# A two-layer token model on one Trainium2 core: values with d on partitions, the norm applied on each head's way out, and a second half whose x stays turned

## The chip, the core and the metric

The program runs on one core of a Trainium2 chip. The metric is device time in microseconds (us) from launch to end, as the median of three runs: 1463.49 us for the kernel before (1462.98 to 1463.92). All data is 32-bit floating point. Engines are named as in the profile: PE (TensorE, matmuls), PEld (TensorE's weight loads), DVE (VectorE), ACT (ScalarE), POOL (GpSimd) and SP (SyncE, which here only issues DMAs).

## The reference, cut to what matters

`x` is 64 batches of 32 tokens with 256 features. Four blocks are added to it in turn. The change touches the first, part of the second, and the third.

Layer 0 attention, for 16 heads of width 128, on `hs = x` mixed by a small matrix per batch:

```python
W2 = where(mask, einsum('bhtm,bhjm->bhtj', qv * enz, es), 0)
o = einsum('bhtj,bhjd->bhtd', W2, v)                    # values
g = hs @ Wg.T
o_n = o * rsqrt(mean(o * o, -1) + 1e-5) * g_norm_weight  # norm over d, one number per token and head
o_g = o_n * silu(g)
x = x + o_g.reshape(B, T, H * 128) @ Wo.T               # all heads summed
```

The norm's factor is one number per token and head, so it commutes with the product by `Wo` of that head.

The second block is a gated MLP with adapters of each batch (rank 16, 8 adapters), then a gated MLP with ternary weights, added to `x`. The third is a linear layer with an adapter of each batch, then attention with 16 heads of width 16:

```python
e = x @ W.T + s[idx] * ((x @ A[idx].T) @ Bm[idx].T)     # rank 16, 8 adapters
q, k, v = split(e @ W_qkv + b_qkv)                      # 16 heads x 16, rotary on the first 4
x = x + softmax(q k^T / 4, causal) v @ W_dense + b_dense
```

The fourth is a product by an expert's matrix of each batch, and a MLP with values rounded to 8-bit steps.

## The kernel before

Tokens are handled in eight chunks of 256 (8 batches, two groups of 128 tokens). The order of the work is written out by hand (`manual_schedule`): each engine takes its instructions in the order in which the Python code emits them. All PSUM results use one pool of eight banks of 128 x 512 (`bank()`); a bank is taken again when the last instruction that uses it, as emitted, is done, and the one released first is taken first.

**First half: `turn(n)`.** Layer 0 attention is cut into 32 steps: 4 groups of four heads, times 8 chunks. `turn(n)` weaves together three or four steps at different stages: `scores`, `attend` and `weigh` of step n; `slots_exp`, `cumsum` and the projections (`project_qk`, L700; `project_vg`, L731) of step n+1 or n; `mix`, `values`, `norm`, `gate`, `turn_og` of step n-1; `leave` of step n-2. What concerns us:

- `values` (L913): the product `w2T^T v`, in 16 matmuls of a 64 x 64 array tile with 128 columns of `v` moving. The result has tokens on partitions and d along the free axis. ACT squares each head and sums along d with `accum_out` (L922).
- `norm` (L929, L931): DVE adds the epsilon, POOL takes the power -1/2 (`f2`).
- `gate` (L943): eight DVE instructions of 128 x 128, each o times `f2` times the gate.
- `turn_og` (L953): eight transposes on PE, and six ACT copies (L957, L960), so that d lies on partitions for the next product.
- `leave` (L968, L973): eight matmuls with 256 moving columns, four heads accumulated in one bank half, and one DVE add of 128 x 512 into `x`.
- `project_vg` for the gate: tokens on partitions, four matmuls of 512 moving columns, and six ACT instructions with Silu.

Beside them, `prepare` (L197 and around) rounds weights for the last block, and `tabulate` copies the adapters of the second block into two tables in DRAM, `alora` and `blora`, from which POOL's indirect DMAs gather each batch's own. `load_mlp` loads the second half's first weights into slots as the attention weights leave them; `chunk_0` runs the start of the second half inside the last turns.

**Second half: `turn2(n)`.** Turn n works on chunk n (adapters, `gate_up`, `down`, `ffn_up`, `ffn_down`, `linear_in`, `linear_adapters`, `linear`), on chunk n-1 (`qkv`, `turn_qk`, `attn_scores`, `attn_exp`, `attn_weights`, `attn_values`, `attn_out`) and on chunk n-2 (`experts_in`, `run_experts`, the last MLP). `drain` finishes chunks 6 and 7. `x` has tokens on partitions, so three times per chunk four PE transposes (L342, through `turned`) turn it: `tokens_in`, `linear_in`, `experts_in`. The linear layer's adapters are all eight at once: `linear_adapters` (L543) multiplies by all 128 ranks, and a DVE multiply with a 0/1 table leaves each batch its own. `qkv` (L1098) makes q, k and v together with tokens on partitions; `turn_qk` (L1136) turns q and k by eight PE transposes.

The weights of the second half (`lw`, `qkvw`, `qkvb`, `dw`, `db`) lie in memory that the first half holds; SP issues their five DMAs when the first half is over (834.5 to 836.9 us).

Of the kernel before, what the change touches and what calls it, by code (L numbers as in the profile page):

```python
# [15 lines left out]
P = 128  # L16
# [9 lines left out]
for _name, _n in (  # L26
    ("ident", 128), ("pair", 64), ("cos", 32), ("sin", 32), ("cos4", 4),
    ("sin4", 4), ("causal", 32), ("blk4", 4), ("adapter", 1), ("p_mod32", 1), ("p", 1), ("p_mod16", 1),
    ("row16", 1), ("head2", 2), ("out_row", 1),
):  # L30
    _CONST[_name] = (_NCONST, _NCONST + _n)
    _NCONST += _n
# [6 lines left out]
def _constants():  # L39
# [25 lines left out]
    put("adapter", p // 16)  # L65
# [10 lines left out]
def mk_kernel(  # L76
# [65 lines left out]
    tables = {}  # L142
    fold = keep.tile([P, P], F32, tag="fold", name="fold")

    def small_tables():
# [20 lines left out]
        m6 = keep.tile([P, B], F32, tag="m6", name="m6")  # L166
        tables["m6"] = m6
        nc.vector.tensor_scalar(m6, idx("lora2"), const("adapter"), scal, ALU.is_equal, MULT)
# [105 lines left out]
    def load_mlp(part):  # L274

        if part == 0:

            for i in range(2):
                mlp["ag", i] = slot(f"ag{i}", [P, 1024])
            mlp["la"] = load(  # L280
                mlp["ag", 0][:, 768:].rearrange("p (c f) -> p c f", c=2),
                laT.rearrange("(c p) f -> p c f", p=P),
            )
            mlp["lbt"] = load(mlp["ag", 1][:, 768:], lb)
        names = {0: (("cgt", 0), ("cut", 0), ("bx", 0)), 1: (("bx", 1), ("cgt", 1)), 2: (("cut", 1), ("cdt", 0))}
        for key in names.get(part, (("cdt", 1),)):
# [8 lines left out]
            else:  # L295
# [3 lines left out]
                    src[:, i * 512 : (i + 1) * 512].rearrange("(c p) f -> p c f", p=P),  # L299
# [4 lines left out]

    alora = dram.tile([8 * P, 192], F32, tag="alora", name="alora")

    blora = dram.tile([8 * P, 2 * P], F32, tag="blora", name="blora")

    def tabulate():
        to = alora.rearrange("(a p) v -> p a v", p=P)  # L310
        pieces = [(ag, k, k * 32) for k in range(2)] + [(au, k, k * 32 + 16) for k in range(2)]
        pieces += [(ad, k, 64 + k * 16) for k in range(8)]
        for src, k, lo in pieces:
            with nc.allow_non_contiguous_dma(reason="ranks of an adapter"):
                nc.sync.dma_start(
                    out=to[:, :, lo : lo + 16], in_=src[k * P : (k + 1) * P, :].rearrange("p (a i) -> p a i", i=16)
                )
            yield
        for r in range(4):
# [36 lines left out]

    def tokens_in(ch):
        c = chunks[ch]
        c["xT"] = turned(lambda gi, k: xq[ch][:, gi, k * P : (k + 1) * P], "xT", first, 2)
# [27 lines left out]
    def fetch_down(ch, gi, held=True):  # L387

        g = ch * 2 + gi
        gather(bdt[:, gi, :], bd, didx[:, g : g + 1], held)  # L390

# [129 lines left out]
    def ffn_down(ch):  # L521
        c = chunks[ch]
        ps = bank()
        for k in range(6):
            for gi in range(2):
                nc.tensor.matmul(  # L526
                    ps[:, gi * D : (gi + 1) * D], lhsT=c["gT"][:, k, gi * P : (gi + 1) * P],
                    rhs=f2w[:, k, :], start=(k == 0 and gi == 0), stop=(k == 5 and gi == 1),
                )
        x = xq[ch].rearrange("p g f -> p (g f)")  # L530
        nc.vector.tensor_tensor(x, ps, x, ADD)

    def linear_in(ch):
        c = chunks[ch]
        c["xT"] = turned(lambda gi, k: xq[ch][:, gi, k * P : (k + 1) * P], "xT", first, 2)

        nc.gpsimd.tensor_tensor(xq[ch], xq[ch], db.unsqueeze(1).to_broadcast([P, 2, D]), ADD)

    def linear_adapters(ch):
        c = chunks[ch]  # L540
        ps = bank()
        for k in range(2):
            nc.tensor.matmul(  # L543
                ps[:, :256], lhsT=mlp["la"][:, k, :], rhs=c["xT"][:, k, :], start=(k == 0), stop=(k == 1)
            )
        xa = big.tile([P, 256], F32, tag="xa", name="xa")
        nc.vector.tensor_tensor(by_batch(xa), by_batch(ps[:, :256]), of_batch(tables["m6"], ch), MULT)
        c["xa"] = xa

    def linear(ch):  # L550
        c = chunks[ch]
        ps = bank()
        for i in range(2):
            for k in range(2):
                nc.tensor.matmul(
                    ps[:, i * 256 : (i + 1) * 256], lhsT=lw[:, k, i * P : (i + 1) * P],
                    rhs=c["xT"][:, k, :], start=(i == 0 and k == 0), stop=False,
                )
        for i in range(2):
            nc.tensor.matmul(  # L560
                ps[:, i * 256 : (i + 1) * 256], lhsT=mlp["lbt"][:, i * P : (i + 1) * P], rhs=c["xa"],
                start=False, stop=(i == 1),
            )
        eT = big.tile([P, 2, 256], F32, tag="eT", name="eT", bufs=2)
        nc.scalar.copy(eT.rearrange("p c t -> p (c t)"), ps)
# [3 lines left out]
    with ExitStack() as s1:  # L569
# [155 lines left out]
        def project_vg(i, which):  # L725
            hq, q, w, hs, lo, s = at(i)
            wt = w[2 if which == "v" else 3]
            for gi in range(2):
                ps = bank()
                for c in range(2):  # L730
                    nc.tensor.matmul(  # L731
                        ps, lhsT=hs[:, c, lo + gi * P : lo + (gi + 1) * P], rhs=wt[:, c, :],
                        start=(c == 0), stop=(c == 1),
                    )
                t = work.tile([P, 512], F32, tag=which, name=which, bufs=2)
                if which == "v":
                    nc.scalar.copy(t, ps)
                else:
                    to, of = by_parity(t), by_parity(ps)
                    nc.scalar.activation(to[:, :, 0, :], of[:, :, 0, :], AF.Silu)  # L740
                    for half in range(2):
                        here, there = slice(half * 64, half * 64 + 64), slice(64 - half * 64, P - half * 64)
                        nc.scalar.activation(to[here, :, 1, :], of[there, :, 1, :], AF.Silu)
                s[which, gi] = t
# [842 lines left out]
```

## Time and profile before

| | us |
|---|---|
| median of three runs | 1463.49 |
| the profiled execution's own time | 1462.34 |
| its span, first to last instruction | 1460.6 |
| PE busy in the span | 1411.5 (97%) |
| PEld / DVE / ACT / POOL busy | 1082.4 / 827.1 / 617.0 / 514.4 |
| one turn of the first half (718.20 to 741.53) | 23.33 |
| one turn of the second half (1080.31 to 1158.10) | 77.79 |
| mean granted TensorE clock | 0.988 |

A row of the profile's groups names a line of the code, the engine, the tiles out<-in, the shape and the count. Every matmul of the code stands in the trace as two records (`values` has 16 matmuls in each of 32 steps, and L913 has 1024 records), a transpose as one (L953: 8 times 32 is 256). Each record has a weight load of its own (PEld). Matmuls are pipelined, so the mean of one is longer than the time from one to the next; the time that a group takes of PE is read from the start of its first record to the start of the next group's first.

### The profile page before, as it was taken

Reading aid. Unit: us, or ns where it says so; the run is one execution under the profiler, and the core shown is the slowest. Engines: PE = TensorE matmul, PEld = TensorE weight load, DVE = VectorE, ACT = ScalarE, POOL = GpSimd, SP = SyncE. Lnnn points to the kernel's source line nnn. Section 1 sums busy time; section 2 is a strip of 40 time slices with the busy share of each in tenths; the row PEclk is TensorE's granted clock in tenths of the full one; section 3 lists DMA queues with packets and bytes.
Section 4 is the critical chain, followed back from the end, with each engine's and each line's share of the span. In section 5 each row is a group of like instructions: output and inputs, shape, how many; then the busy total and the mean of one; then the engine's idle time right before and its main releaser. Section 6 shows DMA issues by size and latency. Waiting matters only on the chain.

```text
span 1460.6 us, 37036 instructions
## 1 busy us (share of the span) xinstructions
PE 1411.5 (97%) x15496; PEld 1082.4 (74%) x15496; DVE 827.1 (57%) x1899; ACT 617.0 (42%) x2014; POOL 514.4 (35%) x586
## 2 busy tenths in 40 slices
PE   5899999999999999999999999999999999999997
PEld 3666777777777777667767878788887878787865
DVE  2566677776768676667565224363636263534555
ACT  1355575656566575746566312121312121222121
POOL 3433243333424243324354243333252515152130
PEclk9999999999999999999999999999999999999999
DMA  6201010100111000100001222122221212121120
GB/s 182 55 2 66 2 30 31 34 2 12 33 39 41 9 9 12 46 2 1 13 16 50 72 79 74 52 73 59 58 75 55 78 38 84 41 73 46 43 77 18
DMA packets 61503, 65.14 MB, mean 45 GB/s; under 512 B 34901, under 2 KB 48853, under 8 KB 61337
## 3 DMA queue, kind: packets, MB, share of 16 engines
q0 software_dynamic: 13312, 35.93, 8.8%
q1 hardware_dynamic: 44824, 22.33, 5.6%
q10 hardware_dynamic: 3200, 4.52, 1.0%
q8 instruction: 122, 2.00, 0.6%
q14 instruction: 45, 0.36, 0.1%
HBM read 60.66 MB, written 3.93 MB: 44 GB/s over the span
## 4 chain that ended last, share of the span: by engine, by line
PE 92%; DMA 2%; DVE 2%; issue 2%; ACT 1%; SPq 1%; POOL 0%; DVEq 0%; POOLq 0%; ACTq 0%
PE ps L700 16%; PE ps L731 15%; PE ps L968 8%; PE ps L436 8%; PE ps L507 5%; PE ps L1301 5%; PE ps L482 3%; PE ps L1341 3%; PE ps L1098 3%; PE ps L526 3%; PE ps L913 2%; PE ps L810 2%; PE ps L450 2%; PE ps L953 2%; PE ps L888 1%
## 5 line engine op out<-in xcount | busy, mean ns | idle before, releaser
L714 POOL TENSOR_TENSOR qT<-ra,rb 128x256 f32<-128x256 f32 x64 | 46.5, 727 | 365.0 <-DVE rb L712 365.0
L922 ACT ACTIVATE sq<-ps 128x128 f32<-128x128 f32 x256 | 70.9, 277 | 213.9 <-PE ps L913 206.8
L368 POOL DMA_INDIRECT we<-in_ew,at x64 | 61.4, 960 | 255.5 <-DVE at L366 170.6
L968 PE MATMUL ps<-wo,ogT 128*128 128x256 f32 x512 | 123.3, 396 | 6.7 <-DVE aT L817 6.7
L700 PE MATMUL ps<-hsT,wq 128*128 128x256 f32 x512 | 126.5, 391 | 0.0
L700 PE MATMUL ps<-hsT,wk 128*128 128x256 f32 x512 | 121.5, 380 | 0.0
L711 DVE TENSOR_TENSOR ra<-ps,ct 128x512 f32<-128x512 f32 x128 | 87.6, 684 | 49.1 <-PE ps L700 44.1
L731 PE MATMUL ps<-wv,hsT 128*128 128x512 f32 x256 | 115.2, 593 | 0.0
L731 PE MATMUL ps<-wg,hsT 128*128 128x512 f32 x256 | 115.1, 592 | 0.0
L968 PEld LDWEIGHTS ps<-wo,ogT 128*128 128x128 f32 x512 | 97.8, 196 | 21.9 <-DVE aT L817 7.3
L700 PEld LDWEIGHTS ps<-hsT,wq 128*128 128x128 f32 x512 | 95.6, 192 | 18.3 <-issue 6.0
L794 DVE RECIPROCAL enz<-ps 128x256 f32<-128x256 f32 x64 | 107.5, 1721 | 1.5 <-PE ps L785 1.5
L700 PEld LDWEIGHTS ps<-hsT,wk 128*128 128x128 f32 x512 | 97.9, 191 | 13.4
L931 POOL TENSOR_TENSOR f<-f,mhalf 128x8 f32<-128x8 f32 x32 | 52.9, 1652 | 132.3 <-DVE f L929 132.3
L731 PEld LDWEIGHTS ps<-wg,hsT 128*128 128x128 f32 x256 | 48.7, 190 | 61.2 <-issue 54.0
L712 DVE TENSOR_TENSOR rb<-ps,ct 128x512 f32<-128x512 f32 x128 | 87.2, 681 | 0.0
L848 ACT ACTIVATE qv<-ok,nmx 128x64 f32<-128x64 f32 x256 | 84.9, 335 | 1.9 <-DVE nmx L844 1.9
L731 PEld LDWEIGHTS ps<-wv,hsT 128*128 128x128 f32 x256 | 48.6, 190 | 47.5 <-issue 45.9
L1301 PE MATMUL ps<-guT,y3T 128*128 128x352 f32 x256 | 79.6, 465 | 1.2 <-ACT y3T L347 1.2
L817 DVE SCALAR_TENSOR_TENSOR aT<-ps,ct 128x256 f32<-128x256 f32 x64 | 24.2, 419 | 86.8 <-PE ps L810 86.8
L458 DVE TENSOR_TENSOR hT<-ps,sg 128x256 f32<-128x256 f32 x64 | 24.3, 420 | 83.5 <-ACT sg L457 83.5
L507 PE MATMUL ps<-yT,f 128*128 128x256 f32 x320 | 71.2, 382 | 0.2 <-ACT yT L493 0.2
(225 smaller groups left out, 2985.3 us busy)
## 6 DMA issues: line engine op xcount, KB each, us to landing
x<-in_x SPq DMA_DIRECT2D x8, 256.0 KB, 9.4
wq<-in_wqT SPq DMA_DIRECT2D x16, 128.0 KB, 2.6
wk<-in_wkT SPq DMA_DIRECT2D x16, 128.0 KB, 3.2
wv<-in_wvT SPq DMA_DIRECT2D x4, 512.0 KB, 10.9
wg<-in_wgT SPq DMA_DIRECT2D x4, 512.0 KB, 3.9
wo<-in_woT SPq DMA_DIRECT2D x4, 512.0 KB, 4.7
row<-in_wgu ACTq DMA_DIRECT2D x11, 128.0 KB, 2.7
out<-res SPq DMA_DIRECT2D x5, 256.0 KB, 2.8
```

What stands on the lines that cost most here:

```text
L368: nc.gpsimd.indirect_dma_start(out=to, out_offset=None, in_=table, in_offset=bass.IndirectOffsetOnAxis(ap=at, axis=0))
L436: nc.tensor.matmul(ps[:, i * 256 : (i + 1) * 256], lhsT=mlp[name, k // 4][:, j, part], rhs=c["xT"][:, j, :], start=(i == 0 and j == 0), st ...
L507: nc.tensor.matmul(ps[:, i * 256 : (i + 1) * 256], lhsT=wt[:, j, k * P : (k + 1) * P], rhs=yT[:, j, :], start=(j == 0), stop=(j == 1),)
L700: nc.tensor.matmul(ps[:, half * 256 : (half + 1) * 256], lhsT=wt[:, c, half * 256 + pr * P : half * 256 + (pr + 1) * P], rhs=hs[:, c, lo : ...
L711: nc.vector.tensor_tensor(by_t(a.rearrange("p h t -> p (h t)")), by_t(ps), cosb, MULT)
L712: nc.vector.tensor_tensor(by_t(b.rearrange("p h t -> p (h t)")), by_t(ps), sinb, MULT)
L731: nc.tensor.matmul(ps, lhsT=hs[:, c, lo + gi * P : lo + (gi + 1) * P], rhs=wt[:, c, :], start=(c == 0), stop=(c == 1),)
L794: nc.vector.reciprocal(t[:, e, :], banks[e][:, :256])
L848: nc.scalar.activation(qv[:, k, :], ok[:, k, :], AF.Exp, bias=nmx[:, k : k + 1], accum_out=rs[:, k : k + 1],)
L922: nc.scalar.activation(sq, po[e][:, k * P : (k + 1) * P], AF.Square, accum_out=f[:, e * 4 + k : e * 4 + k + 1],)
L968: nc.tensor.matmul(ps[:, gi * D : (gi + 1) * D], lhsT=s["ogT", gi][:, h, :], rhs=w[4][:, h, :], start=(h == 0), stop=(h == 3),)
L1301: nc.tensor.matmul(ps[:, :352], lhsT=c["y3T"][:, k, gi * P : (gi + 1) * P], rhs=guT[:, k, lo : lo + 352], start=(k == 0), stop=(k == 1),)
```

## The change

Nothing of the result changes; the work is laid out otherwise.

First half:

- `values` swaps its operands: v is now the weight (64 rows x 128 columns of the array) and `w2T` moves, 64 columns each, so that d lies on partitions. Two ACT instructions square both halves.
- `norm` sums the squares over partitions by eight matmuls with the squares as weight and a single column of ones moving. It is emitted after `project_v`, where before it stood ahead of the last projections.
- `project_g` makes the gate with d on partitions (eight matmuls of 256 columns, two Silu instructions). `gate` multiplies o by it in two DVE instructions, without the norm, and is emitted ahead of the second pair of q/k projections. `turn_og` is gone.
- `leave` keeps heads apart in four banks; eight DVE instructions scale each head by its `f2` while they add it to `x`.

Second half:

- `tokens_in` turns x with features interleaved, and `x` then stays turned: `ffn_down` and `attn_out` produce turned results from weight columns taken with a step of two (`i::2`). `linear_in` and `experts_in` are gone; `tokens_back` turns x back once, before the last add. A third buffer holds a turned x.
- The linear layer has each batch's own adapter. `tabulate` first builds two more DRAM tables, and by 72 gathers on POOL and 24 DMAs on SP the adapters of each chunk (`own_in`, `own_out`), which `fetch_linear` loads per chunk.
- `qkv` becomes `queries_keys` (weights `eT`, 32 array columns each, 128 columns of the q/k weights moving) and `project_values`; q and k are turned by DVE's 32 x 32 transpose instead of PE, and `kb` is made half on ACT, half on DVE.
- The q/k weights are loaded in 32 DMAs of 64-byte pieces, their bias in 16, the values' in three.
- The expert gathers (`fetch`) move later in the turn, and `drain` is put in another order.

```diff
         def values(i):
-                def product(e, rows, out):
-                    nc.tensor.matmul(
-                        po[e][out, k * P : (k + 1) * P], lhsT=s["w2T"][rows, e, k, :],
-                        rhs=s["v", gi][rows, h * P : (h + 1) * P], start=True, stop=True,
-                    )
...
+            for gi in range(2):
+                for h in range(4):
+                    for half in range(2):
+                        rows = slice(64 * half, 64 * half + 64)
+                        k = gi * 4 + h
+                        nc.tensor.matmul(
+                            po[half][:, k * 64 : (k + 1) * 64], lhsT=s["v", gi][rows, h * P : (h + 1) * P],
+                            rhs=s["w2T"][rows, h % 2, gi * 2 + h // 2, :], start=True, stop=True,
+                        )
+            sq = work.tile([P, 8, 2, 64], F32, tag="sq", name="sq", bufs=1)
+            for half in range(2):
+                nc.scalar.activation(
+                    sq[:, :, half, :], po[half].rearrange("p (k t) -> p k t", k=8), AF.Square
+                )
         def norm(i):
+            for gi in range(2):
                 for h in range(4):
+                    to = h % 2 * 4 + gi * 2 + h // 2
                     nc.tensor.matmul(
+                        ps[:, to : to + 1],
+                        lhsT=s["sq"][:, gi * 4 + h, :, :].rearrange("p a t -> p (a t)"), rhs=ones[:, :1],
+                        start=True, stop=True,
                     )
...
         def gate(i):
+            for half in range(2):
+                nc.vector.tensor_tensor(
+                    to[:, half], s["po"][half].rearrange("p (g h t) -> p g h t", g=2, h=4), by[:, half], MULT
+                )
-        def turn_og(i):
...
         def leave(i):
+            for gi in range(2):
+                for pr in range(2):
+                    ps = bank()
+                    for e in range(2):
+                        h = pr * 2 + e
+                        nc.tensor.matmul(
+                            ps[:, e * D : (e + 1) * D], lhsT=s["og"][:, h, gi * P : (gi + 1) * P],
+                            rhs=w[4][:, h, :], start=True, stop=True,
+                        )
+                    for e in range(2):
+                        of = e * 4 + gi * 2 + pr
+                        nc.vector.scalar_tensor_tensor(
+                            xq[q][:, gi, :], ps[:, e * D : (e + 1) * D], s["f2"][:, of : of + 1],
+                            xq[q][:, gi, :], MULT, ADD,
+                        )
...
             more(N)
-            on(n - 1, norm)
+            on(n - 1, gate)
             on(n + 1, project_qk, "q", 1)
             on(n + 1, project_qk, "k", 1)
-            on(n - 1, gate)
             on(n, weigh)
-            on(n, project_vg, "v")
-            on(n, project_vg, "g")
+            on(n, project_v)
+            on(n - 1, norm)
+            on(n, project_g)
...
     def linear_adapters(ch):
+            for j in range(4):
+                nc.tensor.matmul(
+                    ps[32 * j : 32 * j + 32, :64], lhsT=mlp["la"][:, j, k, :],
+                    rhs=c["xT"][:, k, j * 64 : (j + 1) * 64], start=(k == 0), stop=(k == 1),
+                )
     def linear(ch):
+        for gi in range(2):
+            for i in range(2):
+                for k in range(2):
+                    nc.tensor.matmul(
+                        banks[gi][:, i * P : (i + 1) * P], lhsT=lw[:, k, i * P : (i + 1) * P],
+                        rhs=c["xT"][:, k, gi * P : (gi + 1) * P], start=(i == 0 and k == 0), stop=False,
+                    )
+        for i in range(2):
+            for gi in range(2):
+                rows = slice(64 * gi, 64 * gi + 64)
+                nc.tensor.matmul(
+                    banks[gi][:, i * P : (i + 1) * P], lhsT=mlp["lbt"][rows, i * P : (i + 1) * P],
+                    rhs=c["xa"][rows, :, :, :].rearrange("p a b t -> p (a b t)"), start=False, stop=(i == 1),
+                )
...
+    def queries_keys(ch):
+            for b in range(4):
+                for k in range(2):
+                    for i in range(4):
+                        nc.tensor.matmul(
+                            ps[32 * i : 32 * i + 32, b * P : (b + 1) * P],
+                            lhsT=c["eT"][:, k, gi * P + b * T : gi * P + (b + 1) * T],
+                            rhs=wqk[:, k, i, :, :, :].rearrange("p o s d -> p (o s d)"),
+                            start=(k == 0), stop=(k == 1),
+                        )
...
+        nc.vector.transpose(qkT.rearrange("p k s t -> p (k s t)"), flat)
+        nc.scalar.activation(kb[:, :, 0, :], qkT[:, :, 1, :], AF.Copy, scale=const("head2")[:, 0:1])
+        nc.vector.tensor_scalar(kb[:, :, 1, :], qkT[:, :, 1, :], const("head2")[:, 1:2], None, MULT)
+    def project_values(ch):
+                nc.tensor.matmul(
+                    ps[:, gi * 256 : (gi + 1) * 256], lhsT=c["eT"][:, k, gi * P : (gi + 1) * P],
+                    rhs=wv[:, k, :, :].rearrange("p h d -> p (h d)"), start=(k == 0), stop=(k == 1),
+                )
```

## The prediction, made before the result was known

> **What bounds the kernel now.** I read the page's busy shares, then busy time by stretch for one turn of the first half and one of the second, then the timeline of PE inside such a turn, then single groups for prices. Busy shares:
>
> ```profile
> PE 1411.5 (97%) x15496; PEld 1082.4 (74%) x15496; DVE 827.1 (57%) x1899; ACT 617.0 (42%) x2014; POOL 514.4 (35%) x586
> ```
>
> Busy time by stretch (length, then PE, PEld, DVE, ACT, POOL), two turns of the first half and one of the second:
>
> ```profile
> 718.20:741.53 23.33, 23.33 (x262) 17.13 (x260) 14.67 (x29) 14.63 (x53) 10.48 (x13) 1.00 0.03 10
> 741.53:764.86 23.33, 23.33 (x261) 17.13 (x260) 14.66 (x29) 14.63 (x53) 12.36 (x15) 1.00 0.08 21
> ...
> 1080.31:1158.10 77.79, 77.48 (x884) 63.35 (x883) 36.56 (x107) 16.97 (x37) 28.04 (x30) 1.00 0.22 62
> ```
>
> In a steady turn PE is busy all of 23.33 us, at full clock, and DVE, ACT and POOL have 9 us or more free; in the second half PE lacks 0.3 us of 77.79. So the time is the sum of what PE is given; relief on ACT and DVE is worth nothing by itself. The timeline of PE (start, length, line, count) prices each part by start to next start:
>
> ```profile
> 718.63 1.04 PE L953 MATMUL ps<-ct,og 128*128 128x128 f32 x8
> 719.60 0.48 PE L762 MATMUL ps<-ws,rT 17*128 17x256 f32 x2
> ...
> 722.06 3.72 PE L968 MATMUL ps<-wo,ogT 128*128 128x256 f32 x16
> 725.62 1.89 PE L700 MATMUL ps<-hsT,wq 128*128 128x256 f32 x8
> ...
> 729.17 1.10 PE L913 MATMUL ps<-v,w2T 64*64 64x128 f32 x32
> 730.09 0.64 PE L831 MATMUL ps<-es,aT 64*64 64x64 f32 x32
> ...
> 738.10 3.60 PE L731 MATMUL ps<-wg,hsT 128*128 128x512 f32 x8
> 741.53 0.27 PE L871 MATMUL ps<-ct,qe 128*128 128x128 f32 x1
> ```
>
> `turn_og`: 719.60 - 718.63 = 0.97. `values`: 0.92. `leave`: 3.56. The gate's projection: 3.43.
>
> Two more groups decide the case, the only ones with 128-column weights and less than 128 moving columns (timeline again):
>
> ```profile
> 145.97 0.28 PE L222 MATMUL ps<-part,ones 128*128 128x1 f32 x2
> ...
> 1112.64 2.01 PE L450 MATMUL ps<-u,bx 32*128 32x64 f32 x64
> 1114.59 0.56 PE L1301 MATMUL ps<-guT,y3T 128*128 128x352 f32 x1
> ```
>
> L222 is one matmul with one moving column, in two records. A lone record takes 167 ns (the minimum of the group, whose median is 208 and maximum 250), the pair 0.28 us: the second ends 0.11 us after the first although one column streams in no time. L450 has four row tiles of 32, 64 columns each: 64 records in 1114.59 - 1112.64 = 1.95 us, 0.122 us per four.
>
> **What the Trainium skill says.** "TensorE: Matmul & The Clock Gate", section "LDWEIGHTS (loading the stationary operand)": a load takes P/1.2 ns for P weight columns, whatever the rows; 128 columns are 107 ns. Both groups above agree: 0.11 and 0.122 us are a weight load, not the stream. The same page, "The mechanism": a load overlaps running matmuls only where the row groups differ; L450 agrees, since its four row tiles load side by side. "TensorEngine Tiling (Array Packing)", "Instruction Overhead": a matmul with one moving column takes as long as one with 60, so narrowing does not pay there; the 167 ns of L222 for one column fits. The same page, "Key Properties": changing the tiling mode drains the array; the timeline shows about 0.1 us at such a change (1.95 us against 16 loads of 0.112).
>
> **The change, part by part, on PE.** First half, per step:
>
> - `turn_og` leaves: 8 transposes, -0.97.
> - `norm` comes: 8 matmuls of one column, 16 records of 128-column weights, each 0.11 to 0.112: +1.79. It is not hidden: the loads are on one row group and PE has no gap.
> - `values`: again 16 matmuls, but as 64 x 128 tiles only two row groups run side by side instead of four tiles. Streaming stays equal (half the tiles, half the columns), but each tile now loads 128 columns per record: 32 records, two abreast, 16 x 0.112 = 1.79 instead of 0.92: +0.87. No row of before has this shape; the bounds are 0.92 (loads hidden) and 3.58 (no overlap at all). I take 1.79, because L450 shows row groups overlapping and the load setting the pace.
> - `project_g`: 16 records of 256 columns at 0.216 (L700: 1.73 for eight) against 3.43: +0.02. `leave`: 16 records as before, 0.
>
> Sum +1.71 per step, times 32 = +54.7 us.
>
> What else moves in a turn is hidden under PE. DVE: `leave` 8 x 0.38 (L817's shape: two in 0.76) for 0.69, `gate` 2 x 0.68 for 2.15, `e2` three small ones for one: about +1.8 on 14.67 of 25.0. ACT loses six copies, four Silu parts and six squares. POOL's power comes after `qe`, which helps `turn_qe`: `qe` has only 0.24 us in hand before PE needs it (741.29 against 741.53), and about 1 us after. The added wait is PE's on the squares, and `norm` stands 9 us behind `values`. The banks of `leave` were last read by `aT` and `w2T` on DVE, done 1 us earlier. `tabulate` adds 9 gathers of about 1 us in eight turns on POOL, in its idle stretch between `qe` and the next q/k (11 us). If that cover fails, q/k come late by the overrun, but they serve the next turn.
>
> Second half, per chunk: `linear_in` -0.44 and `experts_in` -0.47, `tokens_back` +0.44; `linear_adapters` 0.86 becomes 16 records of 32-column weights, 64 moving, 4 groups of 0.058 and a mode change: -0.53; `linear` base 1.73 becomes 16 records at 0.112: +0.06, its adapter part 0.96 becomes 8 records in pairs, about 0.60: -0.36; `qkv` 5.26 becomes 32 groups of four at 0.11 (3.6) and 8 records of 256 (1.8): +0.14; `turn_qk` -0.87. Sum -2.03, times 8 = -16.2 us. Stepped weights (`i::2`) lie under 256 moving columns, as long as such a load stays below 0.216 (the stepped transposes of `experts_in` paid 0.118 instead of 0.109).
>
> Ends and seams: chunk 0's `linear_in` also waited 0.86, turn 7's `experts_in` 0.5; `drain` puts work into gaps where PE stood 1 us each before `attn_scores`, `attn_out` and `run_experts`: about -3. Against it, SP issues 51 DMAs at 0.35 to 0.51 us from 834.5 us, some 24 us, before `queries_keys` of chunk 0 can run; PE comes to it about 28 us after the first half ends. Landing takes 2 to 3 us, so 0 to 3 us of stall, I take 1. Together -3.5.
>
> Total: 54.7 - 16.2 - 3.5 = +35.0. Against the profiled execution: span 1460.6 + 35 = 1495.6, with 1.7 around it 1497.3; the median of before lies 1.15 above that execution, so 1498.5, said as 1498.
>
> **Rivals.**
>
> - Faster, because weight loads hide. For it: L222's two records start only 28 ns apart, and PEld is busy only 74%. If one-column records cost 0.028 and `values` keeps 0.92, a step changes by 0.45 - 0.97 = -0.5, the first half by -17, and the total is 1463.5 - 17 - 20 = 1427. Against: the ends lie 0.11 apart, and L450. It ends faster as soon as `norm` and the growth of `values` cost under 1.6 us together, instead of 2.66.
> - Half of it: `values` keeps its streaming pace, `norm` pays. Then +0.84 per step, +27 - 20 = +7: 1471.
> - Slower still: a first-half turn is no longer bound by PE alone. `mix` needs `qeT` from ACT, and the 0.97 us of `turn_og` that stood between is gone; or the array's clock drops. For it: before, the clock fell to half twice in the middle of the first half, where `mix` waited about 3 us. At 0.5 to 1 us per turn: +16 to +32, 1515 to 1530. Against: ACT has six copies less ahead of that copy.
> - The change does not do what it says for ACT and DVE: no, it does relieve them, but neither sets the time.
>
> **How the numbers follow.** Forecast 0.82 (own range 1486 to 1508, from the drain, the DMA seam and 0.1 us per step either way), hidden loads 0.05, half 0.04, slower still 0.09. The range, 1481 to 1514, adds the nearer part of the slower case. Three runs of this kernel span 0.06%; about 0.2% is what can be told from no change. Faster 0.05, within 0.2% 0.01, slower 0.94.
>
> **What would show it.** In the changed profile: the one-column group with 512 records, some 57 us busy; `values` near 1.8 us per step; a turn of about 25.0 us with PE still full; a chunk of about 75.8 us. Wrong if the one-column records follow each other in under 0.06 us, if PE shows gaps in the first half, or if a chunk does not shrink.

## The result, and the profile after

The changed kernel takes 1521.32 us (median of four runs, 1517.28 to 1523.61) beside 1463.34 us for the kernel before: ratio 1.0393, 95% interval 1.037 to 1.0415. That is +58 us; the forecast was +35, and 1521 lies above the range. The profiled execution has a span of 1519.7 us, 59.1 more than before, at the same granted clock of 0.988. In part of experiment 5 the kernel before itself took 1551 us, and what ran beside it there is compared with that.

Busy shares of the changed kernel:

```profile
PE 1463.3 (96%) x17064; PEld 1195.4 (79%) x17064; DVE 946.2 (62%) x1975; ACT 481.0 (32%) x1246; POOL 576.8 (38%) x650
```

ACT lost 136 us and the time grew: relief there was worth nothing. PE gained 52 us of busy time, weight loads 113, and DVE 119. Busy time by stretch (length, then PE, PEld, DVE, ACT, POOL), for two turns of the first half and one of the second:

```profile
749.69:774.97 25.28, 25.19 (x280) 20.45 (x276) 18.43 (x32) 10.40 (x30) 10.30 (x13) 1.00 0.04 10
774.97:800.36 25.39, 25.30 (x280) 20.52 (x276) 18.43 (x32) 10.48 (x30) 10.41 (x13) 1.00 0.04 10
1104.00:1180.22 76.22, 76.12 (x1019) 63.91 (x1022) 36.56 (x103) 16.56 (x36) 26.84 (x29) 1.00 0.23 67
```

A turn is still full of PE, and 2 us longer than the 23.33 of before; the undisturbed ones (4, 5, 25 and 26) take 25.18. A chunk of the second half is 1.57 us shorter. The timeline of PE in the first of these turns (start, length, line, count):

```profile
751.51 3.72 PE L1057 MATMUL ps<-wo,og 128*128 128x256 f32 x16
...
758.61 2.00 PE L1008 MATMUL ps<-w2T,v 64*128 64x64 f32 x32
760.54 0.69 PE L920 MATMUL ps<-es,aT 64*64 64x64 f32 x32
...
768.60 1.84 PE L1026 MATMUL ps<-ones,sq 128*128 128x1 f32 x16
770.30 3.70 PE L826 MATMUL ps<-hsT,wg 128*128 128x256 f32 x16
773.84 0.60 PE L966 MATMUL ps<-ct,qe 128*128 128x128 f32 x4
```

From start to next start: `values` 1.93 us (L1008), `norm` 1.70 (L1026), the gate's projection 3.54. The sixteen one-column records of `norm` follow each other in 1.70 / 16 = 0.106 us, although each by itself is shown as 167 to 250 ns long (shortest, median, longest):

```profile
L1026 PE MATMUL ps<-ones,sq x512: 167/250/250, 92.5 to 892.5; 128*128 128x1 f32 x171
```

Where the 59 us came from, stretch by stretch of the two profiled executions (turns are cut at the first record of `scores`, chunks at the adapters of `down`, L466 before and L537 after; the forecast is the prediction's sum, laid on the stretches):

| stretch | before | after | change | forecast |
|---|---|---|---|---|
| start to the first `scores` | 41.8 | 44.5 | +2.7 | 0 |
| turns 0 to 3 | 106.4 | 114.1 | +7.7 | +5.1 |
| turns 4 to 22 | 447.0 | 483.7 | +36.7 | +32.5 |
| turns 23 to 30 | 194.4 | 208.2 | +13.8 | +13.7 |
| rest of the first half | 44.1 | 49.5 | +5.4 | +3.4 |
| chunks 0 and 1 | 130.3 | 127.7 | -2.6 | -3.9 |
| chunks 2 to 6 | 388.9 | 381.1 | -7.8 | -10.2 |
| the last chunk and the drain | 107.7 | 110.9 | +3.2 | -5.5 |

The largest single miss is the last row. PE's waits from 1478 us to the end (who waited, for what, us in total, times, longest):

```profile
PE ps L1435 <- DVE h L204: 7.0, 1, 7.0
PE ps L1451 <- ACT h3T L1438: 1.4, 3, 0.5
```

and the timeline of PE there:

```profile
1482.85 1.93 PE L1381 MATMUL ps<-we,xT 128*32 128x256 f32 x32
1491.77 1.09 PE L1435 MATMUL ps<-ct,h 128*128 128x128 f32 x4 [6.98 <-DVE h L204]
1492.65 0.64 PE L1437 MATMUL ps<-ct,h 128*128 128x128 f32 x2
```

After `run_experts(7)` PE comes straight to `turn_h(6, 1)`, whose `quant_h(6, 1)` stands on DVE behind the rounding of both groups of `y`. PE idles 7 us, and the four transposes after it start 0.22 us apart instead of 0.11: from 1489.0 us on, 6.8 us ran at half the clock. Before, `quant_down(6, 0)` and `quant_up(7, 0)` stood between the two, and the longest waits of PE in the last 37 us were 0.9 and 0.8 us.

### The profile page after: what moved, and what is told of

Its sections match the earlier page's. It is cut to its first block, busy times and chain, and to the rows that moved or that the text cites. A ratio compares the mean times of both kernels' runs of the same rounds, so it can differ in the third digit from the quotient of the medians.

```text
span 1519.7 us, 39665 instructions
## 1 busy us (share of the span) xinstructions
PE 1463.3 (96%) x17064; PEld 1195.4 (79%) x17064; DVE 946.2 (62%) x1975; ACT 481.0 (32%) x1246; POOL 576.8 (38%) x650
## 4 chain that ended last, share of the span: by engine, by line
PE 91%; DVE 2%; SPq 2%; DMA 2%; issue 1%; ACT 1%; POOL 0%; ACTq 0%; DVEq 0%
PE ps L779 15%; PE ps L1057 8%; PE ps L826 7%; PE ps L507 7%; PE ps L809 7%; PE ps L1411 5%; PE ps L1008 4%; PE ps L578 4%; PE ps L1026 4%; PE ps L553 3%; PE ps L1451 3%; PE ps L597 2%; PE ps L899 2%; PE ps L521 2%; SPq L276 2%; PE ps L1219 2%
## 5 line engine op out<-in xcount | busy, mean ns | idle before, releaser
L1057 PE MATMUL ps<-wo,og 128*128 128x256 f32 x512 | 124.4, 398 | 7.5 <-DVE aT L906 6.0
L1063 DVE SCALAR_TENSOR_TENSOR x<-ps,f,x 128x256 f32<-128x256 f32 x256 | 120.9, 482 | 15.2 <-PE ps L1057 3.0
L826 PE MATMUL ps<-hsT,wg 128*128 128x256 f32 x512 | 118.3, 384 | 0.0
L1057 PEld LDWEIGHTS ps<-wo,og 128*128 128x128 f32 x512 | 98.5, 197 | 24.7 <-DVE aT L906 10.8
L1014 ACT ACTIVATE sq<-ps 128x512 f32<-128x512 f32 x64 | 34.8, 595 | 250.1 <-PE ps L1008 250.1
L826 PEld LDWEIGHTS ps<-hsT,wg 128*128 128x128 f32 x512 | 94.9, 190 | 12.0 <-issue 0.5
L937 ACT ACTIVATE qv<-ok,nmx 128x64 f32<-128x64 f32 x256 | 85.3, 334 | 33.6 <-DVE nmx L933 31.5
L1026 PEld LDWEIGHTS ps<-ones,sq 128*128 128x128 f32 x512 | 62.2, 192 | 14.9 <-issue 14.8
```

The lines of the kernel that those rows point to most:

```text
L826: nc.tensor.matmul(ps[:, e * 256 : (e + 1) * 256], lhsT=w[3][:, c, h * P : (h + 1) * P], rhs=hs[:, c, lo : lo + 256], start=(c == 0), stop ...
L937: nc.scalar.activation(qv[:, k, :], ok[:, k, :], AF.Exp, bias=nmx[:, k : k + 1], accum_out=rs[:, k : k + 1],)
L1026: nc.tensor.matmul(ps[:, to : to + 1], lhsT=s["sq"][:, gi * 4 + h, :, :].rearrange("p a t -> p (a t)"), rhs=ones[:, :1], start=True, stop= ...
L1057: nc.tensor.matmul(ps[:, e * D : (e + 1) * D], lhsT=s["og"][:, h, gi * P : (gi + 1) * P], rhs=w[4][:, h, :], start=True, stop=True,)
L1063: nc.vector.scalar_tensor_tensor(xq[q][:, gi, :], ps[:, e * D : (e + 1) * D], s["f2"][:, of : of + 1], xq[q][:, gi, :], MULT, ADD,)
```

## The experiments

Each ratio is against the kernel before, run beside it. A figure in us for a difference is the difference of two ratios times 1463.

**1. Each half of the change alone.** The functions of the other half, and the turns that call them, are before's. One place of many, in the kernel that has the second half alone:

```diff
...
-            on(n, project_v)
-            on(n - 1, norm)
-            on(n, project_g)
+            on(n, project_vg, "v")
+            on(n, project_vg, "g")
...
```

> The second half of the change alone (with its tables), on the first half of before. Theory from the stretches of the two traces: start of the second half +0.6, chunk 1 -3.2, five steady chunks -7.8, end +3.2, so -7 us against before: 1456 (1453 to 1460), if the tables' gathers and DMAs cost the first half nothing. The prediction's own terms, -20 us, would give 1443. If the tables are what made the first half dearer than forecast, 1463 to 1468.

> The first half of the change alone, on the second half of before. Theory: the turns themselves cost 1.85 to 2.1 us more, in all +62 to +66: 1525 to 1530. If the excess over the forecast (54.7 us) belongs to the tables of the second half, which are then absent, 1518. The two halves alone should add up to the whole: +58.

Measured: second half alone 1449.95 us, ratio 0.9927 (0.9912 to 0.9941), -11 us; first half alone 1531.42 us, 1.0488 (1.0471 to 1.0505), +71 us. The sum, +61, is the whole change within the intervals. So the second half is a gain by itself and the first half is the loss, and the tables of the second half did not make it: without them it is not cheaper. Both are some 4 to 5 us further from zero than the stretches said. Turn 24 accounts for most of that: it took 30.6 us before, 26.6 in the second half alone, 33.9 in the first half alone and 31.2 in the whole change. PE waits there for DVE, and DVE for a DMA (experiment 4): PE's wait was 3.5, 2.1, 5.3 and 4.0 us in that order, and 6.8, 0, 6.8 and 3.4 us ran at half clock. An ordinary turn nearby (23.61 or 25.40 us), plus the wait, plus half of the time at half clock, comes to 30.5, 25.7, 34.1 and 31.1 (0.9 short in the second, within 0.2 in the others). Why the transfer is later in one kernel than in another was not settled.

**2. The price of `norm` and of `values`.** First, seven of `norm`'s eight matmuls are left out; the one that stays fills all columns.

```diff
+                    if gi or h:
+                        continue
...
-                        ps[:, to : to + 1],
+                        ps[:, :8],
...
```

> The changed kernel with one of the eight matmuls of norm in each step (the sums of seven heads in eight are left out). Theory, a record costs PE its weight load of 128 columns: 14 records at 0.106 to 0.112 go, 1.5 us per step, -48 us: 1473. Rival, norm's time on PE is a wait for the squares: the wait stays, and the time changes by less than 10 us: 1511 to 1521.

Measured: 1473.85 us, 1.0085 (1.0069 to 1.0101), 45 us less than the whole change. `norm` falls from 1.70 to 0.14 us, the undisturbed turn from 25.18 to 23.98 and most others from 25.40 to 23.99. The time on PE was work, not a wait. Then two versions compute the same sums and products with less of the weight path. In `values` each product is cut along d:

```diff
-                        nc.tensor.matmul(
-                            po[half][:, k * 64 : (k + 1) * 64], lhsT=s["v", gi][rows, h * P : (h + 1) * P],
...
+                        for d in range(2):
+                            to = slice(64 * d, 64 * d + 64)
+                            nc.tensor.matmul(
+                                po[half][to, k * 64 : (k + 1) * 64],
+                                lhsT=s["v", gi][rows, h * P + 64 * d : h * P + 64 * d + 64],
...
```

> The changed kernel with each product of values cut in two along d: 64 x 64 tiles, the same 64 columns moving, twice as many records. Theory, a row group takes its weight columns one after another and the load sets the pace: the columns per row group stay the same number, 16 x 128 per half, whatever the tile, but 64-column loads of the two column groups may lie under one another as in before's values (0.92 us for 32 records of 64 x 64): then 64 records in four groups are 16 x 0.058 = 0.93 to 1.0 us against 1.93, -0.95 per step, -30 us: 1489. Rival, loads of one row group never overlap, so half the columns in twice the records cost the same 1.9 us: 1518 to 1521.

In `norm` ones are the weight, the squares move, and a DVE transpose puts the tokens back on partitions:

```diff
...
+            for j in range(4):
+                t = j % 2 * T
+                nc.tensor.matmul(
+                    ps[32 * j : 32 * j + 32, :256].rearrange("p (k t) -> p k t", k=8), lhsT=ones[:, :32],
+                    rhs=s["sq"][:, :, j // 2, t : t + T], start=True, stop=True,
+                )
+            sums = s["sq"].rearrange("p k a t -> p (k a t)")[:, :256]
+            nc.vector.transpose(sums, ps[:, :256])
...
```

> The changed kernel with the operands of norm exchanged: 32 columns of ones are the weight, the squares move (four column groups of 256 columns each), and DVE turns the sums so that tokens lie on partitions. Theory, norm on PE was paid for its 16 weight loads: now 8 records of 256 columns, four abreast, 2 x 0.216 plus a mode change of 0.1, so 0.45 to 0.6 against 1.70: -1.1 to -1.25 per step, -36 to -40 us: 1482. Rival, the four column groups share one stream and do not run side by side: 8 x 0.216 = 1.73, no change: 1518 to 1523. DVE takes 0.3 to 0.5 us more per step, off PE's path.

Measured: `values` cut, 1489.93 us, 1.0186 (1.0169 to 1.0203), -30 us against the whole change; `norm` by ones, 1486.87 us, 1.0168 (1.0151 to 1.0185), -33 us. The timeline of PE, of the kernel with `values` cut:

```profile
758.08 1.16 PE L1010 MATMUL ps<-w2T,v 64*64 64x64 f32 x64
759.06 0.65 PE L920 MATMUL ps<-es,aT 64*64 64x64 f32 x32
```

and of the one with `norm` by ones:

```profile
767.44 0.64 PE L1025 MATMUL ps<-sq,ones 128*32 128x256 f32 x8
768.01 3.29 PE L826 MATMUL ps<-hsT,wg 128*128 128x256 f32 x14
```

`values` takes 0.98 us instead of 1.93 with twice the records, `norm` 0.57 instead of 1.70. Both rivals fall: the loads of one row group do overlap when they go to different columns of the array, and the four column groups do run side by side. The gain by ones is 3 us short of the expected 36 to 40: the turn fell by 1.02 us (25.18 to 24.16) and not by `norm`'s 1.13, since the projection ahead of it takes 3.52 us instead of 3.44. Both edits together:

> The changed kernel with values in 64 x 64 tiles and norm by a weight of ones, nothing else. Theory, the two products are all of the turn's growth: a turn of 25.18 - 1.0 - 1.02 = 23.16 us (before: 23.33), and the gains add up, 1520 - 30 - 33 = 1457 (1453 to 1460), ratio 0.996. Rival, with PE faster by 2 us the other engines (DVE with 120 us more in the run) become the bound of a turn: 23.6 us or more, 1468 or more.

Measured: 1456.0 us, 0.9964 (0.9955 to 0.9974), 63 us less than the whole change, the sum of the two. Busy time by stretch of that kernel:

```profile
698.50:721.90 23.40, 23.38 (x308) 17.94 (x304) 19.37 (x33) 10.54 (x30) 10.54 (x13) 1.00 0.04 11
721.90:745.20 23.30, 23.23 (x304) 17.81 (x300) 19.46 (x33) 10.44 (x30) 10.43 (x13) 1.00 0.04 10
```

The turn is that of before again (undisturbed 23.16, before 23.19 to 23.33), with DVE at 19.4 us still not the bound. The two products are all of the steady turn's growth.

**3. The order of the end.**

```diff
-        turn_h(6, 0)
-        quant_down(6, 0)
         run_experts(7, (0,))
+        turn_h(6, 0)
         run_experts(7, (1,))
         quant_h(6, 1)
-        turn_h(6, 1)
+        quant_down(6, 0)
         turn_y(7, (0,))
-        quant_down(6, 1)
         quant_up(7, 0)
+        turn_h(6, 1)
         quant_h(7, 0)
...
         quant_up(7, 1)
+        quant_down(6, 1)
```

> The changed kernel with the order of before at the end: quant_down(6,0) and quant_up(7,0) stand between quant_h(6,1) and turn_h(6,1). Theory: the 7.0 us that PE waits for DVE's rounding, and the half clock after it, go: -6 to -8 us, 1514. Rival, DVE sets the end whatever PE's order: the wait turns up at turn_y or turn_h of chunk 7, and the time stays within 2 us of 1521.

Measured: 1510.15 us, 1.0339 (1.032 to 1.0357), 8 us less than the whole change. PE's waits from 1475 us to the end of this kernel:

```profile
PE ps L1411 <- ACT y3T L395: 1.3, 2, 0.8
PE ps L1451 <- ACT h3T L1438: 1.0, 2, 0.5
PE ps L1381 <- DVE xT L1352: 0.6, 1, 0.6
```

The wait of 7 us is gone and not replaced. The last chunk and the drain take 102.8 us, 4.9 less than before; the forecast for the whole end was -5.5. So the order was nearly all of the miss there.

**4. DMAs that DVE waits for, and DMAs on SP.** In turn 3 of the changed kernel the longest wait of DVE, and then PE's, are:

```profile
DVE part L226 <- DMA f<-in_f1T: 7.1, 1, 7.1
```

```profile
PE ps L983 <- DVE aT L906: 4.2, 1, 4.2
```

The masks of `aT` are queued behind a reduction of `f1`, which waits for a load that ACT issues behind the gate's Silu. Turn 24 is alike: DVE waits 6.2 us for a row of `wdown`. The edit issues the three loads after turn 0 and puts the two wide rows, which share one buffer, first and last:

```diff
-        rows += [(wdown[k * P : (k + 1) * P, :], 704) for k in range(2)]
+        downs = [(wdown[k * P : (k + 1) * P, :], 704) for k in range(2)]
+        rows = downs[:1] + rows + downs[1:]
...
             turn(n)
+            if n == 0:
+                next(preparing)
```

> The changed kernel with the loads that prepare needs issued earlier: f1, f3 and f2w after turn 0 instead of at the end of turn 2, and the two wide rows of wdown first and last instead of back to back in one buffer. Theory: DVE, which takes its work in order, waits for these transfers with the masks of aT queued behind it, PE's mix and leave wait for DVE, and the array falls to half clock: turn 3 goes from 32.8 to 25.2 us and turn 24 from 31.2 to about 26, together -10 to -13 us: 1509. Rival: DVE had other late work in these turns, and the waits only change their name: -0 to -4.

Measured: 1509.13 us, 1.0318 (1.03 to 1.0335), -11 us. Turn 3 falls from 32.8 to 25.35 us and turn 24 from 31.2 to 25.84, as expected; turn 12 grows from 27.4 to 31.5, since the first wide row is now loaded just before its use (DVE waits 4.1 us for it). These three turns give 8.6 us. In the traces the stretch before the first `scores`, which the edit was not meant to touch, is 2.1 us shorter as well (42.4 against 44.5), so that the forecast of 10 to 13 us was met in part by luck. The stalls are mostly before's own (its turns 3 and 24 took 28.1 and 30.6): the change added 2.8 us in turn 3 beyond its products. PE waited 4.2 us there instead of 2.5, and 6.8 us instead of 3.4 ran at half clock.

The weights of `queries_keys` and `project_values`, laid out beforehand, so that 4 DMAs take the place of 51:

```diff
...
-        for o in range(2):
-            for which in range(2):
-                for c in range(2):
-                    for i in range(4):
-                        load(
-                            wqk[:, c, i, o, which, :].rearrange("p (h d) -> p h d", h=2),
...
+    load(wqk.rearrange("p c i o s d -> p (c i o s d)"), wqkv[:, :1024])
...
```

> The changed kernel with the weights of queries, keys and values laid out beforehand, so that 4 DMAs take the place of 51. Theory: SP's 37 us of issuing end before PE comes to queries_keys and project_values of chunk 0, the stall of 2 to 3 us there goes: 1518 (-2 to -3.5). Rival: PE waits there for eT or a bank and nothing changes: within 1 us of 1521.

Measured: 1516.44 us, 1.0369 (1.0351 to 1.0386). The interval overlaps that of the whole change, so the time alone decides nothing. The trace does: in the changed kernel's timeline of PE,

```profile
934.22 0.67 PE L1255 MATMUL ps<-wv,eT 128*128 128x256 f32 x2
936.64 1.56 PE L1255 MATMUL ps<-wv,eT 128*128 128x256 f32 x6 [1.75 <-DMA wv<-in_wqkv]
```

and with packed weights:

```profile
932.24 1.89 PE L1237 MATMUL ps<-wv,eT 128*128 128x256 f32 x8
```

The wait is gone, and `queries_keys` of chunk 0 takes 3.63 us, against 3.94.

**5. All mends together, with the new first half and with before's.** The first kernel has all edits of experiments 2 to 4, and the first two rows loaded early too; the second has before's first half with the mends of 3 and 4.

> The changed kernel with values in 64 x 64 tiles, norm by a weight of ones, the end in the order of before there, the loads of prepare early (its first two rows too, which the run before this one left behind as a wait of 4 us in turn 12) and the four packed DMAs. Theory, the gains lie on different stretches of PE's path and add up: 1520 - 30 - 33 - 11 - 4 - 8 - 3.5 = 1430 (1426 to 1435), a turn of 23.2 us. Rival, the added work on DVE meets the other waits, and a part of the gains is lost: 1436 to 1450.

> The first half of before (values with tokens on partitions, norm on DVE and POOL, turn_og on PE) with the second half of the change and the same three mends (end, early loads, packed DMAs). Theory: the second half alone gave 0.9927 of before, 1452 on this scale; the end gives 8, the DMAs 3, the loads 8 to 10: 1431 (1427 to 1436). A turn stays at 23.33 against 23.2 in the other kernel of this pair, so it ends 3 to 7 us later than that one; if the layout of the change costs more than its two products, it ends earlier.

Measured: 1631.3 and 1630.5 us, where the kernel before took 1550.9: ratios 1.0526 (1.05 to 1.0552) and 1.0529 (1.0504 to 1.0554). The same two kernels, run again:

> The same kernel as best_new, again: in that call the kernel before itself took 1551 us instead of 1461 to 1463, and in the turns with POOL's gathers DVE and ACT stood still for some 12 us with nothing released in the profile. Theory: that belongs to the chip in that hour, not to the edits. Where before takes 1463 again, this one takes 1430 (1426 to 1435), ratio 0.978. Rival: the edits themselves (the early loads, the packed weights) bring the stalls: then again a ratio above 1.02.

> The same kernel as best_old, again, with before's first half. Theory as there: 1431 to 1436, ratio 0.979 to 0.982, 3 to 7 us behind the other of this pair, since a turn takes 23.33 us here and 23.2 there. Rival as in the other of this pair: the stalls come from the edits that both share, ratio above 1.02.

Again 1633.8 and 1630.0 against 1551.7: 1.0532 and 1.0519. The timeline of a long turn of the first kernel shows what stood:

```profile
203.75 0.95 POOL L434 DMA_INDIRECT staged<-blin,lidx  x1 [0.30 <-issue]
204.90 1.41 SPq L352 DMA_DIRECT2D own_in<-staged  x2
206.47 0.55 SPq L358 DMA_DIRECT2D own_out<-staged  x1
206.67 0.76 DVE L992 TENSOR_TENSOR w2T<-ps,ct 128x256 f32<-128x256 f32 x2 [8.38 <-remote]
206.73 1.21 ACT L854 ACTIVATE es<-ps 128x256 f32<-128x256 f32 x4 [12.48 <-remote]
```

DVE and ACT start again together, 0.2 us after SP begins to issue the DMA that takes the last of POOL's nine gathers onward; the profile names no releaser on this core. PE is touched too: while the gathers began, its 32 records of `mix` came in six pieces, 0.2 to 0.4 us apart. Turns 6 to 13, which hold these gathers, take 31 to 36 us and turns 27 to 30, with the gathers of the second half's adapters, 27 to 30; nearly all other turns take 23. The second half lost nearly as much: chunks 2 to 6 take 84 to 88 us each instead of 76.2, and 87 of the 197 us between this execution and the shorter one of the same kernel below lie in it. The second half's gathers are before's as well, and before lost some 89 us in these runs; no trace of before was kept there, so that the two losses are the same is likely and not shown. The same gathers at the same pace (1.25 us each) held up nothing in the traces of experiment 4. With before at 1461 us again, and with the 72 gathers left out (plain loads stand in their place):

> The kernel of best_new, where the kernel before takes 1463 again: 1430 (1426 to 1435), ratio 0.978. If the stalls of the two calls before belong to the edits and not to the chip in that hour, a ratio above 1.02 again.

> The kernel of best_old, where the kernel before takes 1463 again: 1431 to 1436, ratio 0.979 to 0.982, 3 to 7 us behind best_new3. If the new layout costs more than its two products, it ends ahead of it.

> The kernel of best_new without the 72 gathers of the first half (two plain loads per chunk of the linear layer's second matrix stand in their place, so the adapters of the linear layer are not the batches' own). The prediction's step, that the gathers lie in POOL's idle time: within 3 us of best_new3. Rival, they hold up DVE and ACT as in the calls where before took 1551 us, there by some 12 us in each of eight turns: -10 us or more against best_new3, up to -95.

Measured, beside 1461.45 us for before: the new first half 1432.62 us, 0.9803 (0.9782 to 0.9825); before's first half 1435.68 us, 0.9823 (0.9803 to 0.9842); without the 72 gathers 1431.35 us, 0.9804 (0.978 to 0.9828). So the rival that the edits bring the stalls falls, the gains add up, and the gathers are all but free there: turns 6 to 13 take 189.6 us with them and 187.5 without, which the whole times do not resolve. The two first halves cannot be told apart at these intervals; most turns are 23.16 to 23.38 us in one and 23.19 to 23.62 in the other. Both kernels are about 2% faster than before. What made the gathers so dear where before took 1551 us stays open: no kernel without gathers ran there. The record gives the chip the same number, 7, in those runs and in experiment 4, where before took 1462 us, so it need not be a property of one chip.

## Why the prediction was wrong

Direction and mechanism held: PE full, weight loads on the path, relief on ACT and DVE worth nothing. What failed is the sum, 24 us short. The largest term in it is the order of `drain`, which was forecast as a gain and was a loss; the other terms were mis-sized or put at nothing:

- **"`drain` puts work into gaps", "about -3".** This step failed (-5.5 forecast for the whole end, +3.2 measured: 8.7 us). The prediction counted what the new order fills and never asked what each PE instruction then finds ready. In the code, `quant_h(6, 1)` stands on DVE behind the two roundings of `run_experts`, with nothing on PE between `run_experts` and `turn_h(6, 1)`. Experiment 3 gives 8 us back. (The four terms of the ends as given, -0.86, -0.5, -3 and +1, also make -3.4 and not -3.5.)
- **The turn, "+1.71 per step".** `norm` was forecast +1.79 and is +1.70; `values` forecast 1.79 and is 1.93, so +1.01 instead of +0.87. The gate's projection is +0.11 instead of +0.02, `turn_qe` and `attend` are +0.09 and +0.06, `mix` -0.15, `turn_og` -0.97 as said. Sum +1.85, which is 25.18 - 23.33; in the nine turns 14 to 22 it is +1.79 (23.61 to 25.40). Over 32 steps that is 2.6 to 4.5 us more than forecast. That the misses of `norm` and `values` nearly cancel was luck.
- **DVE, "about +1.8" per turn.** It was +3.8 (14.67 to 18.43): each of `leave`'s eight took 0.48 us, not 0.38, and the three small `e2` 1.8 us together (see the last section). It cost nothing, since PE stayed the bound.
- **"0.1 us per step either way" for stalls.** Turn 3 is 2.8 us longer than its products explain (wait and half clock, experiment 4) and turn 12 1.2 us (PE waits 2.0 us for DVE there instead of 0.7); turn 24 is 1.3 us shorter. The prediction saw the two falls of the clock in before's first half and did not follow them to their cause, DVE's wait for a DMA. The last `leave` at half clock (5.34 us instead of 3.56) is most of the miss in the rest of the first half; no wait stands before it (last section).
- **The chunk, "-2.03".** Measured -1.57. `linear`'s base is +0.25 (forecast +0.06), and parts that no term named moved: `attn_values` +0.23, `adapters_spread` +0.11, `attn_out` +0.09, `adapters_in` -0.22. The adapters of the linear layer -0.50, its second product -0.31, queries, keys and values +0.10, and the transposes (-0.87, and three turns of `x` made two, -0.43 together) came near what was worked out. Over five chunks 2.3 us.
- **The DMA seam, "+1".** 1.75 us of wait and 0.3 of a slower `queries_keys`; right in kind, half of the size. The issue of the 51 DMAs took 31.7 us (903.4 to 935.1), not "some 24".
- **The start, 0.** It was 2.7 us longer in this execution. The first half alone, without tables, starts at 41.7 us, but the kernels with tables start anywhere from 41.7 to 45.2; whether the change has a part in it is open.
- **The gathers, 0.** Right to within some 2 us, by the last run of experiment 5, where before takes 1461; far from right in the runs where before took 1551 us, which no term foresaw.

The rivals: loads that hide are excluded by 0.106 us per record, half of it by the 1.93 us of `values`, and both by experiment 2. "Slower still" named 1515 to 1530, and the time is there, but for other reasons: `mix` takes 0.69 to 0.91 us in ordinary turns, as it did before, so it does not wait longer for `qeT`, and the mean clock is unchanged. A trace of it shows only once PE gets faster: `norm` with one matmul takes 1.56 us less of PE, the turn only 1.2 to 1.4 less.

What the prediction drew from the Trainium skill: for weight loads of full columns the price of 107 ns held (16 records at 0.106 us). The sentence of "TensorE: Matmul & The Clock Gate", "The mechanism", that loads overlap only where row groups differ, is narrower than what was measured. "TensorEngine Tiling (Array Packing)", "Key Properties", says that different tiles load and multiply in parallel; the cut `values` agrees, since its four 64-column loads, two in each row group, pass in 0.98 / 16 = 0.061 us, which leaves no room for two one after the other (by the first page's price an estimated 0.107). The drain at a change of tiling mode was read as "about 0.1 us"; the numbers given for it (1.95 against 16 times 0.112) leave 0.16. "TensorEngine Tiling (Array Packing)", "When to Use Tiling", names the exchange of operands for a narrow moving side, with column tiles: that is `norm` by ones, 0.57 us.

## What to carry to other kernels

On a path bound by TensorE, price a matmul by its moving columns or by its weight columns, whichever takes longer (here 128 weight columns and one moving column took 0.106 us a record, 256 moving columns 0.216). Where the moving side is narrow, exchange the operands or cut the weight into column tiles before giving up the layout: here that took 63 us out of a change that cost 58. When instructions are put in another order, write for each one what it waits for on its neighbours' in-order queues; one transpose put before its rounding cost 8 us. A stall costs PE its wait and half of the time at half clock after it (turn 24). Where PE is full, as here, a layout that frees ACT and DVE is worth what it takes from PE, and no more: with every mend made, the new first half and before's cannot be told apart.

## What the runs showed of the hardware

- Column tiles of one row group load weights side by side: 64 records of 64 x 64 in 0.98 us, 32 of 64 x 128 in 1.93 (experiment 2).
- A DVE instruction with both inputs in SBUF did not end before the POOL instruction that ran beside it. Groups of DVE in the changed kernel:

```profile
L957 DVE SCALAR_TENSOR_TENSOR e<-rs 64x4 f32<-64x4 f32 x64 | 42.8, 669 | 2.0 <-ACT qv L937 1.2
L954 DVE SCALAR_TENSOR_TENSOR e<-rs 128x4 f32<-128x4 f32 x32 | 15.2, 475 | 1.6 <-ACT qv L937 1.6
L1032 DVE SCALAR_TENSOR_TENSOR f<-ps,e 128x8 f32<-128x8 f32 x32 | 5.3, 166 | 7.8 <-PE ps L1026 6.9
```

Four columns take 0.67 us, while the instruction with one input in PSUM takes 0.17. In the timeline the DVE instruction and POOL's end together, at 769.95 and 769.94:

```profile
769.21 0.73 POOL L794 TENSOR_TENSOR qT<-ra,rb 128x256 f32<-128x256 f32 x1
769.47 0.48 DVE L954 SCALAR_TENSOR_TENSOR e<-rs 128x4 f32<-128x4 f32 x1
```

Of the 32 instructions of L954, 31 run beside `qT` and end 0.02 us after it; the one with POOL idle takes 0.163 us. Of the 64 of L957, 62 end so after `kT`. `norm` by ones gives the comparison, since there L1032 reads both inputs from SBUF:

```profile
L1032 DVE SCALAR_TENSOR_TENSOR f<-sq,e 128x8 f32<-128x8 f32 x32 | 22.1, 691 | 1.1
```

Thirty of these run beside POOL's `qe` and take 0.72 to 0.73 us, the two with POOL idle 0.173; with an input in PSUM the line takes 0.165 to 0.168 beside the same `qe`. Before's `e2` (median 0.16) started just ahead of the end of POOL's `kT`. "GPSIMD Engine Reference", "1. Specifications", says that POOL's SBUF interface is shared with VectorE, with contention for instructions that have two SBUF inputs; these numbers agree.
- The clock can fall to half although PE has no gap. Ahead of the last `leave`, 3.7 us of PE go to matmuls with 1 and 64 moving columns:

```profile
890.96 1.84 PE L1026 MATMUL ps<-ones,sq 128*128 128x1 f32 x16
892.73 2.01 PE L521 MATMUL ps<-u,bx 32*128 32x64 f32 x64
894.67 5.41 PE L1057 MATMUL ps<-wo,og 128*128 128x256 f32 x16
```

From 895.1 us on the clock was half for 3.4 us, and this `leave` took 5.34 us instead of 3.56. In the traces the clock changes only at steps that lie 3.41 us, or a multiple of it, apart. The same fall stands in five kernels (the changed one, `values` cut, and the three with the new order of the end, the early loads and the packed weights), and in each the 3.4 us before it held almost nothing but these two groups. It is absent in the first half alone, where the same two groups were shared between two steps, and in the kernels whose `norm` is short. So few moving columns seem to count as idleness for the clock; no run varied that alone.
- In part of experiment 5 the kernel before took 1551 us instead of 1461 to 1463, and in the changed kernels DVE and ACT stood during gathers. Measure before beside every run.
